# Two graph-attention layers: second block's adjacency in the setup, and a few steps of the layer change reordered

## The chip, the cores and the metric

The kernel runs on one core of a Trainium2 chip. The metric is the device time of one execution in microseconds, the median of several runs. TensorE (PE in the profile) multiplies matrices and transposes; VectorE (DVE), ScalarE (ACT) and GpSimd (POOL) work elementwise; SyncE (SP) only issues transfers and passes on waits. Each engine takes its own instructions in the order in which the program lists them, and semaphores make one engine wait for another. Matmuls write to PSUM banks, from which VectorE and ScalarE read.

## The reference, cut to what matters

Eight batches of 2048 nodes with 256 features pass through two layers; both use one adjacency matrix of 2048 x 2048. All arithmetic is float32.

```
# layer 0: attention in chunks, 4 heads of 64
h = relu(layernorm(x))
q, k, v = h Wq' + bq, h Wk' + bk, h Wv' + bv
for each of 8 chunks of 256 keys:                # softmax inside a chunk
    s = clip(q k' / 8, -10, 10);  s = -10 where adj == 0
    ctx += softmax(s) v
x = x + layernorm(ctx Wo' + bo + h) * gamma + beta
# layer 1: graph attention, one head
h = relu(layernorm(x)) W
e = leaky_relu(e_src[:, None] + e_dst[None, :], 0.01);  e = -1e9 where adj == 0
x = x + relu(softmax(e) h)
```

## The kernel before

**Blocks and steps.** The 2048 nodes of a batch are four blocks of 512 (`NNB`), each of four tiles of 128 (`TB`). Layer 0's attention walks 32 steps (`Attention.STEPS`), each one block of queries against one chunk of keys; every step is cut into two halves, `begin(f)` and `end(f)`, so that half steps are numbered 2f and 2f+1. Work that isn't attention is hung on half steps through the dictionary `todo`: a piece marked "first" runs at the head of its half step, one marked "pe" among TensorE's matmuls, the rest between the clips and the exponentials. The schedule is the order in the program; nothing reorders it.

**Adjacency.** A half row is 128 nodes x 1024 neighbours, 512 KB of int32. `load_rows` fetches it into one of four buffers; `missing_of` (L203, DVE) makes a mask of it; `turn_missing` (L211, PE, eight transposes into a bank of ps_t) turns it; `keep_bounds` (L215, ACT) writes it as int8 into `bounds[nb]`, the upper bound that `clip` (L440) uses for block nb. A block has eight half rows. Before, the setup treats block 0's half rows, two beside each projection block; `adjacency(nb)` spreads those of blocks 1, 2 and 3 over the half steps of batch 0's attention, block 1's from the first on. `store_bounds` saves the int8 blocks to DRAM for the later batches.

**Projections.** `Projection` computes q, k and v of a block: `load` brings x (two buffers), `stats`, `power` and `shift` give mean and scale (DVE, ACT, DVE), `norm(nb, t2)` normalizes half a block (L282, ACT), `turn` transposes it (L291, PE) and copies the two halves (L330 on DVE, L332 on ACT), `qk` multiplies (L344) and copies each product with its bias (L348, ACT); its `part` 0 is q, 1 is k. `values` is L358, with an addition on DVE (L363). With `ps_h` the products go to the large banks ps_s, otherwise by turns to ps_n and ps_t, two buffers of each.

**First attention step.** `Attention.early(0..2)` runs the first logits (L400), their clips (L440) and exponentials (L449) ahead of the step loop. In batch 0 all three stand behind the whole setup; in the others among the products of layer 1.

**The layer change.** When the attention of a batch ends, TensorE works through an order written by hand: for each of the four blocks (`zero`, `low`, `mid`, `last`) the output product (`output` L598, `take` L607), normalization, and then layer 1's transposes and copies (`ends(0)`: `turn1` L291, `keep1` L665 on ACT) and products with the weight W (`ends(1)`: `values` L672, `keep` L680 on ACT and L681 on DVE). Between them stand the next batch's projections (`ahead`). Then come the aggregation's inputs: `targets` (L764, L765), `sources` (L772 transposes, L776), `mean`, `weights` (L782 and L788 on DVE), and the aggregation itself (`products`, L805). The last batch has no `ahead`, and an order of its own. The sum over chunks is gathered by a transfer that adds (`gather`, L475), which the output products wait for.

**Fences.** Where two groups of matmuls write one bank, SyncE carries the wait (L372), in the same queue as its transfers.

Of the kernel before, what the change touches and what calls it, by code (L numbers as in the profile page):

```python
# [28 lines left out]
def gnn_two_layers(  # L29
# [26 lines left out]
    TB = NB // P  # L56
    NNB = N // NB
# [58 lines left out]
    bounds, bounds1 = {}, {}  # L116

    def bound_tile():
        return xpool.tile([P, NT, NB], I8, tag="bound", name="bound", bufs=2)
# [6 lines left out]
    def store_bounds(nb):  # L126
        nc.sync.dma_start(bound_d[nb], bounds[nb])
# [11 lines left out]
    def row_bcast(src, name):  # L139
        t = const.tile([P, F], F32, name=name)  # L140
        nc.sync.dma_start(t, row(src))
        return t
# [19 lines left out]
    def pe(piece):  # L162

        piece.kind = "pe"
        return piece
# [29 lines left out]
    def load_rows(t, half):  # L195
        rows = xpool.tile([P, HALF], I32, tag="x", name="rows", bufs=NNB)
        nc.sync.dma_start(rows, adj[t * P:(t + 1) * P, half * HALF:(half + 1) * HALF])
        return rows

    def missing_of(rows, t, half):  # L200

        z = work.tile([P, HALF], BF16, tag="hn", name="z", bufs=5)
        nc.vector.tensor_scalar(  # L203
            z, rows, 0.0, 0.0, op0=ALU.is_equal, op1=ALU.add, accum_out=missing[:, t, half:half + 1]
        )
        return z

    def turn_missing(z):
        pt = ps.tile([P, 8, P], BF16, tag="t", name="ps_z")
        for k in range(8):  # L210
            nc.tensor.transpose(pt[:, k, :], z[:, k * P:(k + 1) * P], ident_b)  # L211
        return pt

    def keep_bounds(pt, t, half):
        nc.scalar.activation(  # L215
            bounds[t // TB][:, half * 8:(half + 1) * 8, (t % TB) * P:(t % TB + 1) * P], pt, AF.Copy,
            scale=-2.0 * CLIP * SC, bias=CLIP * SC,
        )
# [622 lines left out]
    proj = Projection(0)  # L841
# [6 lines left out]
    bk_c = column(bk, "bk_c")  # L848
    bv_r = row_bcast(bv, "bv_r")
    proj.load(1)  # L850
    nearest = [(t, half) for t in range(TB) for half in range(2)]
    rows = {i: load_rows(*nearest[i]) for i in range(4)}
    proj.stats(0, range(TB))
    proj.power(0)
# [8 lines left out]
    bo_r = row_bcast(bo, "bo_r")  # L863
    gamma_r = row_bcast(gamma, "gamma_r")
    beta_r = row_bcast(beta, "beta_r")
    found = {i: missing_of(rows.pop(i), *nearest[i]) for i in range(2)}
    bounds[0] = bound_tile()
    proj.stats(1, range(TB))
    proj.power(1)
    proj.shift(1)  # L870
    for nb in range(NNB):
        for i in (2 * nb, 2 * nb + 1):
            keep_bounds(turn_missing(found.pop(i)), *nearest[i])
            if i + 4 < len(nearest):
                rows[i + 4] = load_rows(*nearest[i + 4])
        if nb + 1 < NNB:
            proj.norm(nb + 1, 0)
        proj.qk(nb, bank=ps_h)
        if nb + 1 < NNB:
            proj.norm(nb + 1, 1)  # L880
            for i in (2 * nb + 2, 2 * nb + 3):
                found[i] = missing_of(rows.pop(i), *nearest[i])
            if nb + 2 < NNB:
                proj.load(nb + 2)
            proj.turn(nb + 1, 0)
            proj.turn(nb + 1, 1)
            if nb + 2 < NNB:
                proj.stats(nb + 2, range(TB))
                proj.power(nb + 2)
                proj.shift(nb + 2)  # L890
        proj.values(nb)

    def layer1_weight():
        nc.sync.dma_start(w1s[:, :, 0:F], w1.rearrange("(c p) f -> p c f", p=P))

    def layer1_vector(i):
# [9 lines left out]

    once = {
        1: [lambda: raws.update(o=load_output_weight(wo)), layer1_weight],
        2: [lambda: store_bounds(0)],
        5: [pe(lambda: turn_weight(raws["o"], woT))],  # L910
        6: [lambda: layer1_vector(0)],
        7: [lambda: layer1_vector(1)],
        HALVES - PER: [find_lone],
    }
    for nb in range(1, NNB):
        for n, pieces in sorted(adjacency(nb).items()):
            once.setdefault(max((nb - 1) * PER + n, 0), []).extend(pieces)
    for piece in once.pop(0):
        piece()

    projs = {0: proj, 1: Projection(1)}
    projs[1].adder = nc.gpsimd
    att = Attention(proj)
    for part in range(3):
        att.early(part)
    unfinished = None
    for b in range(B):
        sd = small.tile([P, 2, NT], F32, tag="sd", name="sd", bufs=2)
# [2 lines left out]
        zero, low, mid, last = blocks  # L931
        ahead = projs.get(b + 1)
# [5 lines left out]
        def at(n, *pieces):  # L938
            todo.setdefault(n, []).extend(pieces)
# [7 lines left out]
        def fetch(of, nb):  # L947
            of[nb] = fetch_bounds(nb)
# [4 lines left out]
        if b == 0:  # L953
            for n, pieces in once.items():
                at(n, *pieces)

            for nb in range(NNB):
                n = 12 * nb + 5
                at(n - 2, lambda nb=nb: ahead.load(nb))
                for t in range(TB):  # L960
                    at(n + t, lambda nb=nb, t=t: ahead.stats(nb, [t]))
                at(n + 4, lambda nb=nb: ahead.power(nb))
                at(n + 5, lambda nb=nb: ahead.shift(nb))
        else:
            at(6, lambda: fetch(bounds, 1))
            at(PER + 4, lambda: fetch(bounds, 2))
            at(2 * PER + 4, lambda: fetch(bounds, 3))
# [39 lines left out]

        for block in blocks:
            block.adder = nc.vector
        for t in range(TB):  # L1010
            mid.stats1([t])
            low.values(t)
            low.keep(t)
        mid.power1()
        mid.shift1()
        if ahead:
            ahead.load(2)
            ahead.turn(1, 0)
            ahead.turn(1, 1)
            mid.norm1(0)  # L1020
            mid.norm1(1)
            ahead.norm(2, 0)
            ahead.values(0)
            last.output(0)
            last.output(1)
            last.take(0)
            last.take(1)
            ahead.norm(2, 1)
            ahead.load(3)
            mid.ends(0)  # L1030
            last.stats(range(TB))
            ahead.qk(1, 0)
            last.power()
            last.shift()
            last.scaled(range(TB))
            ahead.qk(1, 1)
            for t2 in range(2):
                last.gamma(t2)
                last.add(t2)
            for t in range(TB):  # L1040
                last.stats1([t])
                mid.values(t)
                mid.keep(t)
            last.power1()
            last.shift1()
            ahead.turn(2, 0)
            ahead.turn(2, 1)
            last.norm1(0)
            last.norm1(1)
            ahead.values(1)  # L1050
            zero.norm1(0)
            zero.norm1(1)
            ahead.norm(3, 0)
            ahead.qk(2, 0)
            zero.ends(0)
            zero.ends(1)
            ahead.norm(3, 1)
            ahead.qk(2, 1)
            ahead.turn(3, 0)
            ahead.turn(3, 1)  # L1060
            ahead.values(2)
            last.ends(0)
            last.ends(1)
            one.total()
            ahead.qk(3, 0)
            one.targets()
            one.sources(0)
            one.sources(1)
            ahead.qk(3, 1)
            weights(0)  # L1070
            one.mean()
            weights(1)
            ahead.values(3)
        else:
            mid.norm1(0)
            mid.norm1(1)
            one.targets(TB, 2 * TB)
            weights(0)
            mid.ends(0)
            last.output(0)  # L1080
            last.output(1)
            last.take(0)
            last.take(1)
            mid.ends(1)
            last.stats(range(TB))
            last.power()
            last.shift()
            weights(1)
            last.scaled(range(TB))
            one.targets(2 * TB, 3 * TB)  # L1090
            accs[0] = one.accumulators(0)
            early(0)
            for t2 in range(2):
                last.gamma(t2)
                last.add(t2)
            last.stats1(range(TB))
            last.power1()
            last.shift1()
            weights(2)
            last.norm1(0)  # L1100
            last.norm1(1)
            early(1)
            last.ends(0)
            last.ends(1)
            early(2)
            one.total()
            one.targets(3 * TB, NT)
            one.sources(1)
            weights(3)
            one.mean()  # L1110
            weights(4)

        far = projs[b + 2] = Projection(b + 2) if b + 2 < B else None
        for i, (nb, j4) in enumerate(pieces1):
# [19 lines left out]
            if far and i in (1, 3, 6, 9):  # L1134
                n = (1, 3, 6, 9).index(i)
# [3 lines left out]
            if ahead and i == len(pieces1) - 4:  # L1139
                att = Attention(ahead)  # L1140
# [36 lines left out]
```

## Time and profile before

| | us |
|---|---|
| median of 3 runs (lowest, highest) | 3664.26 (3662.63, 3664.51) |
| profiled span | 3661.2 |
| first attention matmul (L400) | 70.55 |
| first product of layer 1's aggregation (L805), batch 0 | 432.16 |
| the same, last batch | 3533.97 |

The page gives each engine's busy time with its share of the span. A timeline line gives the start in us, the length in us, the engine, the source line, the tiles written and read, how many instructions were merged, and in brackets how long the engine had stood idle and which engine and line released it. A line of the waits gives the total in us, how often, and the longest. TensorE's instructions overlap, so the spacing of two starts tells more than one instruction's length.

### The profile page before, as it was taken

What the parts mean: (1) busy time and instruction counts of PE and PEld (TensorE: products, weight loads), DVE (VectorE), ACT (ScalarE), POOL (GpSimd) and SP (SyncE); (2) the same over time, 40 slices, a digit from 0 to 9 for tenths busy, and PEclk for the clock granted to TensorE, in tenths of its full rate; (3) what the DMA queues carried; (4) which work ended last, traced back from release to release, by engine and by line L of the source; (5) the groups of instructions that cost most, each with busy time, mean ns of one, the idle gap of its engine ahead of it and who ended that gap; (6) DMA issues with size and microseconds to landing.
All of it is one profiled execution on the core that took longest, in us unless ns stands there. A gap on an engine that the chain in (4) does not pass through costs nothing.

```text
span 3661.2 us, 99422 instructions
## 1 busy us (share of the span) xinstructions
PE 3624.1 (99%) x43952; PEld 2209.7 (60%) x43952; DVE 2582.2 (71%) x3915; ACT 1959.1 (54%) x2975; POOL 1788.7 (49%) x1142
## 2 busy tenths in 40 slices
PE   8999999999999999999999999999999999999999
PEld 4444784547745577445775558645586555865468
DVE  4887577865778666776667856678576784767766
ACT  4777416773267732677236762367713766147650
POOL 0678016870178602786037850378404774048731
PEclk9999999999999999999999999999999999999999
DMA  4554113340134411343113431134312432124321
GB/s 141 137 129 111 41 52 83 83 109 26 67 80 89 94 42 52 83 100 82 47 47 83 100 76 46 59 77 95 75 52 59 88 88 59 47 53 89 71 59 35
DMA packets 116641, 274.83 MB, mean 75 GB/s; under 512 B 9968, under 2 KB 75248, under 8 KB 108016
## 3 DMA queue, kind: packets, MB, share of 16 engines
q0 software_dynamic: 32256, 117.45, 17.6%
q1 hardware_dynamic: 83952, 151.01, 12.1%
q8 instruction: 344, 5.64, 0.6%
q14 instruction: 89, 0.73, 0.1%
HBM read 130.03 MB, written 20.97 MB: 41 GB/s over the span
## 4 chain that ended last, share of the span: by engine, by line
PE 95%; DVE 2%; ACT 1%; DMA 1%; issue 0%; POOL 0%; POOLq 0%; SPq 0%; DVEq 0%; ACTq 0%
PE ps_s L400 24%; PE ps_n L416 23%; PE ps_s L805 12%; PE ps_t L428 6%; PE ps_n L805 6%; PE ps_t L805 6%; PE ps_t L598 3%; PE ps_s L344 2%; PE ps_n L344 2%; PE ps_t L344 2%; PE ps_t L672 2%; PE ps_t L358 1%; PE ps_n L672 1%; PE ps_n L358 1%; PE ps_t L291 1%; DMA ctxT<-prod 1%
## 5 line engine op out<-in xcount | busy, mean ns | idle before, releaser
L455 POOL TENSOR_TENSOR both<-e 128x1024 f32<-128x1024 f32 x512 | 1217.8, 2407 | 667.7 <-PE ps_s L400 269.9
L440 DVE SCALAR_TENSOR_TENSOR e<-ps_s,bound 128x1024 f32<-128x1024 f32 x1024 | 1219.4, 1220 | 384.8 <-PE ps_s L400 383.8
L400 PE MATMUL ps_s<-q,k 64*32 64x512 f32 x16384 | 1364.9, 590 | 2.8 <-DVE e L440 2.6
L449 ACT ACTIVATE e<-e 128x1024 f32<-128x1024 f32 x1024 | 1050.6, 1049 | 560.8 <-DVE e L440 540.5
L416 PE MATMUL ps_n<-e,v 64*32 64x512 f32 x16384 | 1164.0, 590 | 2.4 <-DVE prod L470 2.4
L416 PEld LDWEIGHTS ps_n<-e,v 64*32 64x32 f32 x16384 | 447.0, 107 | 501.7 <-issue 395.5
L400 PEld LDWEIGHTS ps_s<-q,k 64*32 64x32 f32 x16384 | 433.5, 106 | 460.3 <-issue 325.8
L822 POOL TENSOR_TENSOR x<-x,r 128x256 f32<-128x256 f32 x128 | 98.5, 769 | 1148.3 <-DVE rz L815 1017.4
L428 PE MATMUL ps_t<-both,ones 64*32 64x512 f32 x4096 | 537.5, 591 | 1.0 <-SPq L372 0.5
L805 PE MATMUL ps_s<-g,w 128*128 128x257 f32 x2048 | 448.6, 380 | 0.0
L470 DVE TENSOR_TENSOR prod<-ps_n,rz 128x512 f32<-128x512 f32 x448 | 288.7, 686 | 189.3 <-PE ps_n L416 85.1
L805 PEld LDWEIGHTS ps_s<-g,w 128*128 128x128 f32 x2048 | 387.8, 190 | 55.5
L788 DVE SCALAR_TENSOR_TENSOR w<-bound,w 128x1024 f32<-128x1024 int8 x256 | 313.7, 1225 | 8.7
L805 PE MATMUL ps_n<-g,w 128*128 128x257 f32 x1024 | 292.4, 382 | 0.0
L782 DVE TENSOR_SCALAR w<-src,cd 128x512 f32<-128x512 f32 x512 | 265.3, 561 | 36.2 <-ACT src L776 35.8
L805 PE MATMUL ps_t<-g,w 128*128 128x257 f32 x1024 | 289.8, 380 | 0.0
L460 ACT ACTIVATE rz<-ps_t 128x512 f32<-128x512 f32 x256 | 152.5, 596 | 172.3 <-PE ps_t L428 92.6
L475 POOL DMA_DIRECT2D ctxT<-prod x224 | 194.2, 867 | 52.5 <-DVE prod L470 49.0
L805 PEld LDWEIGHTS ps_n<-g,w 128*128 128x128 f32 x1024 | 192.2, 190 | 43.8 <-issue 17.6
L805 PEld LDWEIGHTS ps_t<-g,w 128*128 128x128 f32 x1024 | 193.9, 189 | 28.2
L428 PEld LDWEIGHTS ps_t<-both,ones 64*32 64x32 f32 x4096 | 121.1, 106 | 93.7 <-SPq L372 53.0
L461 ACT ACTIVATE rz<-rz 128x512 f32<-128x512 f32 x256 | 161.4, 631 | 8.1
(129 smaller groups left out, 2854.0 us busy)
## 6 DMA issues: line engine op xcount, KB each, us to landing
ctxT<-prod POOLq DMA_DIRECT2D x224, 512.0 KB, 4.9
bound<-bound_d SPq DMA_DIRECT2D x60, 1024.0 KB, 5.3
xp<-in_x_dram SPq DMA_DIRECT2D x60, 512.0 KB, 4.8
rows<-in_adj_dram SPq DMA_DIRECT2D x32, 512.0 KB, 5.3
x<-in_x_dram SPq DMA_DIRECT2D x32, 512.0 KB, 5.3
out_dram<-x SPq DMA_DIRECT2D x31, 512.0 KB, 2.9
bound_d<-bound SPq DMA_DIRECT2D x4, 1024.0 KB, 6.0
out_dram<-x SPq DMA_DIRECT2D x4, 128.0 KB, 1.7
```

The lines of the kernel that those rows point to most:

```text
L344: nc.tensor.matmul(pp, w[:, di, do * P:(do + 1) * P], self.hT[nb][:, di, :], start=di == 0, stop=di == FC - 1,)
L400: nc.tensor.matmul(self.s[n, o][c * Q:(c + 1) * Q, kt, :], self.k[p][rows, at:at + Q], self.q[p][rows, nb * NB:(nb + 1) * NB], start=True, ...
L416: made.append(nc.tensor.matmul(self.num[n, c][h * Q:(h + 1) * Q, :], self.v[rows, j * KT + kt, at:at + Q], self.e[n, p][rows, i * KT + kt, :],
L428: nc.tensor.matmul(self.total[n][h * Q:(h + 1) * Q, :], ones[rows, :], self.both[n, h // 2][rows, h % 2, :], start=half == 1, stop=half == 0,)
L440: nc.vector.scalar_tensor_tensor(self.e[n, p][:, i * KT:(i + 1) * KT, :], self.s.pop((n, o)), -CLIP * SC, bounds[nb][:, j * KT:(j + 1) * K ...
L449: nc.scalar.activation(e, e, AF.Exp, scale=1.0 / SC)
L455: nc.gpsimd.tensor_tensor(self.both[n, p], e[:, 0], e[:, 1], op=ALU.add)
L470: nc.vector.tensor_tensor(dst[:, c, :], self.num.pop((n, c)), self.rz[n], op=ALU.mult)
L475: nc.gpsimd.dma_start(self.ctxT[nb], self.prod.pop(n), accum_op=ALU.add)
L782: nc.vector.tensor_scalar(w[:, i, :], self.src[nb], self.cd[:, 0, j:j + 1], self.cd[:, 1, j:j + 1], op0=ALU.mult, op1=ALU.max,)
L788: nc.vector.scalar_tensor_tensor(two, bounds1[nb][:, j - 1:j + 1, :], 0.0, two, op0=ALU.is_gt, op1=ALU.mult)
L805: nc.tensor.matmul(accs[t][:, 0:F + 1], w[:, i, t * P:(t + 1) * P], g[:, j, :], start=j == 0, stop=j == NT - 1,)
```

## The change

It does four things. The setup treats the half rows of block 0 and of block 1, four beside each projection block instead of two, with q and k of a block parted (`find` makes masks and loads the row four places on, `bound` turns and keeps). The three early parts of batch 0's first attention step go among the projections of its last block. In the last batch, block `low`'s products run together before block `mid` is normalized, and block `last`'s output product goes ahead of `mid`'s transposes. In the layer change of the other seven batches two pieces of projection go between a block's transposes and its products. The statistics of batch 1, which are taken during batch 0, move from every twelfth half step to every fourth, into the room that block 1's half rows leave.

```diff
-    nearest = [(t, half) for t in range(TB) for half in range(2)]
+    nearest = [(t, half) for t in range(2 * TB) for half in range(2)]
...
+    find(0, 1)
+    for nb in range(2):
+        bounds[nb] = bound_tile()
     proj.stats(1, range(TB))
     proj.power(1)
     proj.shift(1)
-    for nb in range(NNB):
-        for i in (2 * nb, 2 * nb + 1):
-            keep_bounds(turn_missing(found.pop(i)), *nearest[i])
-            if i + 4 < len(nearest):
-                rows[i + 4] = load_rows(*nearest[i + 4])
-        if nb + 1 < NNB:
-            proj.norm(nb + 1, 0)
-        proj.qk(nb, bank=ps_h)
-        if nb + 1 < NNB:
-            proj.norm(nb + 1, 1)
-            for i in (2 * nb + 2, 2 * nb + 3):
-                found[i] = missing_of(rows.pop(i), *nearest[i])
-            if nb + 2 < NNB:
-                proj.load(nb + 2)
-            proj.turn(nb + 1, 0)
-            proj.turn(nb + 1, 1)
-            if nb + 2 < NNB:
-                proj.stats(nb + 2, range(TB))
-                proj.power(nb + 2)
-                proj.shift(nb + 2)
+    for nb in range(NNB - 1):
+        bound(4 * nb, 4 * nb + 1)
+        proj.norm(nb + 1, 0)
+        proj.qk(nb, 0, ps_h)
+        find(4 * nb + 2, 4 * nb + 3)
+        proj.norm(nb + 1, 1)
+        bound(4 * nb + 2, 4 * nb + 3)
+        proj.qk(nb, 1, ps_h)
+        find(4 * nb + 4, 4 * nb + 5)
+        if nb + 2 < NNB:
+            proj.load(nb + 2)
+        proj.turn(nb + 1, 0)
+        proj.turn(nb + 1, 1)
+        if nb + 2 < NNB:
+            proj.stats(nb + 2, range(TB))
+            proj.power(nb + 2)
+            proj.shift(nb + 2)
         proj.values(nb)
+    bound(12, 13)
+    proj.qk(NNB - 1, 0, ps_h)
+    att = Attention(proj)
+    att.early(0)
+    find(14, 15)
+    proj.qk(NNB - 1, 1)
+    att.early(1)
+    bound(14, 15)
+    proj.values(NNB - 1)
+    att.early(2)
...
-        2: [lambda: store_bounds(0)],
+        2: [lambda: store_bounds(0), lambda: store_bounds(1)],
...
-    for nb in range(1, NNB):
+    for nb in range(2, NNB):
         for n, pieces in sorted(adjacency(nb).items()):
...
-                n = 12 * nb + 5
-                at(n - 2, lambda nb=nb: ahead.load(nb))
+                n = 4 * nb + 4
+                at(n - 3, lambda nb=nb: ahead.load(nb))
...
             zero.ends(0)
-            zero.ends(1)
             ahead.norm(3, 1)
             ahead.qk(2, 1)
+            zero.ends(1)
             ahead.turn(3, 0)
             ahead.turn(3, 1)
             ahead.values(2)
             last.ends(0)
+            ahead.qk(3, 0)
             last.ends(1)
             one.total()
-            ahead.qk(3, 0)
             one.targets()
             one.sources(0)
...
         else:
+            mid.stats1(range(TB))
+            low.ends(1)
+            mid.power1()
+            mid.shift1()
             mid.norm1(0)
             mid.norm1(1)
             one.targets(TB, 2 * TB)
             weights(0)
-            mid.ends(0)
             last.output(0)
             last.output(1)
             last.take(0)
             last.take(1)
+            mid.ends(0)
             mid.ends(1)
```

More of the change, by code (lines that the diff above doesn't have):

```diff
@@ L865, in gnn_two_layers, with find, bound @@
     beta_r = row_bcast(beta, "beta_r")
-    found = {i: missing_of(rows.pop(i), *nearest[i]) for i in range(2)}
-    bounds[0] = bound_tile()
+    found = {}
+    def find(*parts):
+        for i in parts:
+            found[i] = missing_of(rows.pop(i), *nearest[i])
+            if i + 4 < len(nearest):
+                rows[i + 4] = load_rows(*nearest[i + 4])
+    def bound(*parts):
+        for i in parts:
+            keep_bounds(turn_missing(found.pop(i)), *nearest[i])
+    find(0, 1)
+    for nb in range(2):
+        bounds[nb] = bound_tile()
     proj.stats(1, range(TB))
@@ L914, in gnn_two_layers @@
     }
-    for nb in range(1, NNB):
+    for nb in range(2, NNB):
         for n, pieces in sorted(adjacency(nb).items()):
             once.setdefault(max((nb - 1) * PER + n, 0), []).extend(pieces)
-    for piece in once.pop(0):
-        piece()
     projs = {0: proj, 1: Projection(1)}
     projs[1].adder = nc.gpsimd
-    att = Attention(proj)
-    for part in range(3):
-        att.early(part)
     unfinished = None
@@ L1009, in gnn_two_layers @@
             block.adder = nc.vector
[L1010 to L1015, printed above, removed]
-        if ahead:
+        if ahead:
+            for t in range(TB):
+                mid.stats1([t])
+                low.values(t)
+                low.keep(t)
+            mid.power1()
+            mid.shift1()
             ahead.load(2)
@@ L1074, in gnn_two_layers @@
         else:
+            mid.stats1(range(TB))
+            low.ends(1)
+            mid.power1()
+            mid.shift1()
             mid.norm1(0)
```

## The prediction

> **What bounds the kernel now.** I read the page first, then the list of waits, then the timeline at the three places that the change touches.
>
> ```profile
> PE 3624.1 (99%) x43952; PEld 2209.7 (60%) x43952; DVE 2582.2 (71%) x3915; ACT 1959.1 (54%) x2975; POOL 1788.7 (49%) x1142
> ...
> PE 95%; DVE 2%; ACT 1%; DMA 1%; issue 0%; POOL 0%; POOLq 0%; SPq 0%; DVEq 0%; ACTq 0%
> ```
> TensorE is busy for 99% of the span and is 95% of the chain that ended last. So an edit pays only where TensorE stands still, or where a matmul waits in a way that stretches a group. The change removes no matmul. It can win only holes in TensorE's row.
>
> ```profile
> PE ps_t L291 <- ACT hn L282: 9.5, 12, 3.2
> PE ps_t L672 <- ACT hT L665: 6.1, 15, 0.5
> ```
> These lines of TensorE's waits (total, times, longest) name two holes: layer 1's products (L672) wait for the copy of their transposed input (15 times, which is 7 layer changes x 2 and one more), and transposes (L291) wait for the normalization. Here is one layer change, TensorE alone:
>
> ```profile
> 402.42 0.60 PE L291 MATMUL ps_n<-ident,hn 128*128 128x128 f32 x4
> 403.50 1.28 PE L672 MATMUL ps_t<-w1s,hT 128*128 128x258 f32 x4 [0.48 <-ACT hT L665]
> ...
> 407.23 1.88 PE L344 MATMUL ps_t<-hT,wkT 128*128 128x512 f32 x4
> ...
> 415.43 0.60 PE L291 MATMUL ps_n<-ident,hn 128*128 128x128 f32 x4
> 416.37 1.28 PE L672 MATMUL ps_t<-w1s,hT 128*128 128x258 f32 x4 [0.34 <-ACT hT L665]
> ...
> 420.10 1.88 PE L344 MATMUL ps_t<-hT,wqT 128*128 128x512 f32 x4
> ```
> The setup, where each block's transposes wait for ScalarE:
>
> ```profile
> 24.94 0.38 PE L291 MATMUL ps_t<-ident,hn 128*128 128x128 f32 x2
> 26.37 0.33 PE L291 MATMUL ps_t<-ident,hn 128*128 128x128 f32 x1 [1.05 <-ACT hn L282]
> ...
> 27.46 1.89 PE L358 MATMUL ps_t<-wvT,hT 128*128 128x256 f32 x8
> ```
> And the end of the last batch:
>
> ```profile
> 3518.15 1.03 PE L672 MATMUL ps_n<-w1s,hT 128*128 128x258 f32 x4
> 3522.33 1.95 PE L291 MATMUL ps_t<-ident,hn 128*128 128x128 f32 x4 [3.15 <-ACT hn L282]
> ...
> 3524.93 3.62 PE L598 MATMUL ps_t<-woT,ctxT 128*128 128x256 f32 x8
> 3528.34 2.29 PE L598 MATMUL ps_n<-woT,ctxT 128*128 128x256 f32 x8
> ...
> 3533.97 14.04 PE L805 MATMUL ps_s<-g,w 128*128 128x257 f32 x64
> ```
> The reader is to see, beside the hole of 3.15 us, that the first eight output products (L598) take 3.41 us to the next group, where eight of the same shape take 1.73 us at an ordinary layer change. TensorE is slow just after the hole.
>
> [...] 3.41 against 1.73 us is a factor of two, after 3.15 us of idleness and then sparse transposes; the 1.05 us holes of the setup are followed by nothing slow. [...] so a copy queued behind a waiting instruction waits too, which is how I place every wait below.
>
> **Part 1: the layer change (seven times).** The products of block 0 go behind the second half of block 2's projections (k), and those of block 3 behind the first half of block 3's (q). Nothing is added. First hole: the transposes' last group starts at 402.42 and needs 0.44 us (the group before it began at 401.98), so TensorE could go on at 402.86; L672 starts at 403.50, 0.64 us later, and its 16 matmuls take 3.73 us (403.50 to 407.23), where four such groups without a wait take 3.49 us (390.73 to 394.22 in the same view): 0.24 more. Second hole: 415.87 to 416.37 is 0.50, and again 3.73 instead of 3.49. Sum 0.64 + 0.24 + 0.50 + 0.24 = 1.62 us. In the new order a projection half (2 x 1.72 us) stands between transposes and products; the two copies need 2 x 0.8 us on ScalarE, so they are hidden. Does the projection find its banks? It takes the banks of the projection half before the transposes, whose copies end at 402.13 and 402.87, against a need at 402.86 and 404.6. On ScalarE the normalization (1.08 us) now stands ahead of the k copies; they end near 405.7 and 407.2, and the products need those banks at 408 and 408.9. After block 3's products the transposes of the sources follow at once and read only other blocks' columns; the targets on ScalarE wait 0.8 us for the last column, and behind them stand the source exponentials. The weights then start about 2.1 us after the sources' transposes, 1.8 before, and are needed 8.6 us after them: hidden. So 7 x 1.62 = **11.3 us gained**. Bounds: 8 (if half of the 0.24s and a little more stay) to 12.
>
> **Part 2: the setup.** Removed: the transposes of a block take 24.94 to 27.46 = 2.52 us instead of 0.88, since ScalarE normalizes after four copies; now the second normalization stands between the q and k halves. 1.64 x 3 = 4.9 us gone. Moved in: block 1's eight half rows. Each costs DVE 1.21 us (L203), TensorE 0.5 (16 transposes in 1.0), ScalarE 1.01 (L215). TensorE's work only moves: 4 us more in the setup, 4 us less later. Per block ScalarE has about 10 us, DVE 10, TensorE 13.5 (7.0 projections, 3.5 values, 0.9 transposes, 2.0 masks): TensorE stays the fullest, so what matters is order.
>
> The added wait: SyncE's queue. In the new order two row loads stand before each load of x, and each must wait until the mask of the row four places before has freed its buffer. I walk the queues: DVE makes masks 2 and 3 from 18.0 to 20.3 as before, then masks 4 and 5 to 22.7; the load of x for block 2 goes out at 23 instead of 15.33 and lands at 28.7 (4.8 us from the page's DMA part, and 0.9 for the row loads ahead of it, each 1.45 us as 512 KB at the 361 GB/s of the stretch 10 to 20). Statistics take 2.35 us (27.83 to 30.05), the scale factors on ScalarE and the shift 1.1, the value addition behind them on DVE 0.69: 32.9. That addition frees the bank of the next block's second mask. TensorE: q to 21.5, masks 22.5, k 26.0, transposes 26.9, values 30.35, first mask 30.8: a stall of 2.1 us, where before it was 0.35. For block 3 the same walk gives x out at 38.9, landed at 43.9, the addition at 47.9, TensorE there at 46.2: 1.75. So of 4.9 us some 3.2 come back.
>
> The early attention: its first 32 matmuls now lie between q and k, which hides their clips; before, 1.40 and 0.56 us were lost there, and 0.66 and 0.36 on the masks. But the third part still waits for clip (0,2), which stands on DVE behind the last value addition: 2.1 us; the values wait for a mask copy that stands on ScalarE behind two exponentials, 1.2 us; the first logits wait 0.5 us for a q copy and the second step's 1.2 us for a clip. That is 5 us, hardly less than before. In times: q of block 3 from 61.9 (60.08 before) to 65.3, first logits to 67.7, k to 71.2, second logits 72.9, masks 73.9, values from 75.1 to 78.65, its addition 79.5, clip (0,2) 80.8, the second step's first logits 81.6, its last from 83.2 to 84.6; before they ended at 84.34. By then eight more half rows are done instead of four (the others came at 108.59 and 117.56): 2.2 us gained.
>
> Later in batch 0 the statistics of batch 1 move from every twelfth to every fourth half step. Before, their last two blocks fell together with block 3's masks, with single holes: 0.56 us at 201.07, 0.48 at 251.07, and near 265. They now fall where block 1's masks were: 1.8 us gained. Part 2 together: **4 us gained**. Best case 9 (x arrives in time), worst a loss of 5 (each load of x 3 us later still, and the tail's waits doubled).
>
> **Part 3: the last batch's end.** The output products go ahead of block 2's transposes. They need the last accumulating transfer into ctxT: issued at 3517.14, 4.8 us to land as the one before (3510.61), so 3522.0; the hole is 3519.0 to 3522.0, hardly shorter. But dense products follow it at once instead of transposes that come one by one. If the clock stays up: 16 products 3.46 to 3525.4; transposes 0.88 to 3526.3; a wait of 0.6 for the copy (and for the takes on DVE, which come after the weights at 3526.0 and end at 3527.4); products 3.7, to 3530.6, instead of 3533.97. **3.4 us gained**; what follows hangs on these products through DVE's chain and moves with them. If the clock falls: 1 us.
>
> **The rivals.** (a) Main line: 3664.3 - 11.3 - 4 - 3.4 = 3645.6. (b) The same with the clock falling at the end: 3648; [...] against it, the 2.4 us of sparse work near 3549 slowed nothing. (c) Setup takes back what it wins, the x loads late: +9 against the main line, 3654.6; for it, DMA engines are full from 10 to 20 us. (d) Setup without new stalls: 3640.6; for it, TensorE is the fullest engine there. (e) The other side: the reordered projections wait for their banks and the hole of 0.9 us only moves, once in each change (7 x 0.9 = 6 more, none gained), the setup loses 5, the end gains nothing: 3664 + 6 + 5 = 3675; against it stand the copies' times of part 1.
>
> **How the numbers follow.** Chances: (a) 0.46, (b) 0.2, (c) 0.15, (d) 0.15, (e) 0.04. The likeliest is (a): 3645.6 us. The range must hold (a), (b), and most of (c) and (d): 3639 to 3655. Within 0.2% means above 3657: the upper part of (c) and some of (e), 0.06; slower 0.04; faster 0.9.
>
> **What would show it.** Right: no L672 behind L665 at the layer changes, spans between changes shorter by 1.6 us; in the setup, TensorE waiting for DVE's L363 instead of ACT's L282, second step's logits ending near 84 us; L598 ahead of L291 at the end, with 1.73 us for eight. Wrong: new waits of L344 at the changes, first attention later than 90 us, or L598 still at 3.4 us.

## The result and the profile after

| | before | after |
|---|---|---|
| median of 6 runs each, us (lowest, highest) | 3663.19 (3660.94, 3664.51) | 3653.97 (3649.28, 3656.7) |
| ratio, 95% interval | | 0.9973 [0.996, 0.9986] |
| profiled span, us | 3661.2 | 3650.6 |

The change makes the kernel faster, by 9.2 us where 18.7 were forecast. The time lies at the upper end of the range, beside rival (c), 3654.6: the setup takes back what it wins because the loads of x come late. TensorE's share of the span and of the chain that ended last is what it was (first two lines of the page on engines and of its chain):

```profile
PE 3613.9 (99%) x43952; PEld 2203.8 (60%) x43952; DVE 2581.0 (71%) x3915; ACT 1958.1 (54%) x2975; POOL 1788.5 (49%) x1142
...
PE 95%; DMA 2%; DVE 2%; ACT 1%; POOL 0%; issue 0%; SPq 0%; POOLq 0%; DVEq 0%; ACTq 0%
```

TensorE's waits (engine, tile and line, releaser: total us, times, longest) show what went and what came. The 15 waits of L672 are two, and the 9.5 us of L291 are 2.7. At the head stands one that was 0.4 us before, also in two waits: the transposes of masks wait for the value addition, 8.4 us now.

```profile
PE ps_z L211 <- DVE v L363: 8.4, 2, 5.9
...
PE ps_t L291 <- ACT hn L282: 2.7, 5, 1.5
PE ps_t L598 <- DMA ctxT<-prod: 2.6, 1, 2.6
...
PE ps_t L672 <- ACT hT L665: 0.7, 2, 0.3
```

Where the difference of the two spans arose, by the times at which some matmuls start:

| stretch | before, us | after, us | difference | forecast |
|---|---|---|---|---|
| start to the first L416 (context of the first step) | 84.34 | 92.81 | +8.47 | +0.3 |
| from there to batch 0's first L805 | 347.82 | 341.75 | -6.07 | -5.6 |
| from there to the last batch's first L805 | 3101.81 | 3087.51 | -14.30 | -13.1 |
| from there to the end | 127.23 | 128.52 | +1.29 | 0 |

The forecasts are those of the prediction: 84.6 instead of 84.34; 2.2 + 1.8 and one layer change of 1.62; six layer changes and 3.4 for the last batch's end. The second and third rows came about as forecast. The first did not. Here is the setup after, TensorE alone:

```profile
30.66 0.61 PE L211 MATMUL ps_z<-ident_b,z 128*128 128x128 bf16 x8
37.19 1.01 PE L211 MATMUL ps_z<-ident_b,z 128*128 128x128 bf16 x8 [5.91 <-DVE v L363]
37.99 4.83 PE L344 MATMUL ps_s<-hT,wqT 128*128 128x512 f32 x8
...
54.46 1.01 PE L211 MATMUL ps_z<-ident_b,z 128*128 128x128 bf16 x8 [2.48 <-DVE v L363]
55.27 4.72 PE L344 MATMUL ps_s<-hT,wqT 128*128 128x512 f32 x8
...
82.99 1.99 PE L358 MATMUL ps_t<-wvT,hT 128*128 128x256 f32 x8 [0.70 <-ACT bound L215]
...
88.63 2.19 PE L400 MATMUL ps_s<-q,k 64*32 64x512 f32 x24 [1.91 <-DVE e L440]
91.89 1.49 PE L400 MATMUL ps_s<-q,k 64*32 64x512 f32 x20 [1.07 <-DVE e L440]
```

Two holes stand in the places that were forecast, but of 5.91 and 2.48 us instead of 2.1 and 1.75, and the q projection after each takes 4.83 and 4.72 us, where the one without a hole takes 3.65. The granted clock is why: it stood at 0.50 from 33.52 to 40.35 and from 54.01 to 57.42, and at 1.00 between and behind. In this line (stretch, length, busy us of PE, PEld, DVE, ACT and POOL with their counts, granted clock, DMA share, GB/s) it is the third number from the end:

```profile
36.94:40.34 3.40, 3.15 (x11) 1.92 (x11) 3.40 (x7) 2.30 (x4) 0.00 (x0) 0.50 0.12 13
```

Follow the first hole back. VectorE:

```profile
33.30 0.43 DVE L259 BATCH_NORM_STATS2 stats<-xp 128x6 f32<-128x256 f32 x1 [5.63 <-DMA xp<-in_x_dram]
...
36.36 0.16 DVE L270 TENSOR_TENSOR krn<-krn,mv 128x4 f32<-128x4 f32 x1 [0.84 <-ACT krn L266]
36.44 0.69 DVE L363 TENSOR_TENSOR v<-ps_t,bv_r 128x512 f32<-128x512 f32 x1
```

VectorE stood idle for 5.63 us until block 2's x was there. The value addition, whose products were done at 29.10 and 30.83, stands behind the statistics in its order and starts at 36.44; when its first half ends, the bank is free and the mask's transposes start, at 37.19. SyncE's own queue says when that x was asked for:

```profile
14.93 9.33 SPq L197 DMA_DIRECT2D rows<-in_adj_dram  x6
24.35 0.39 SPq L151 DMA_DIRECT2D xp<-in_x_dram  x1
```

It went out at 24.35 and landed at 33.27. Ahead of it three row loads were still under way; by the trace they landed at 27.02, 29.06 and 30.33, in the order of their issue. In the trace the landing of each of these loads is reported in sixteen parts: fifteen parts of x were in by 31.71, and the last, 1.56 us later, is what VectorE waited for. Why it came so late no run here shows. The table by stretches gives the rate meanwhile (the second stretch runs on past the landing):

```profile
24.00:28.00 4.00, 4.00 (x18) 2.49 (x17) 0.69 (x1) 3.74 (x6) 0.00 (x0) 1.00 0.82 233
28.00:34.00 6.00, 3.27 (x22) 2.73 (x21) 0.67 (x3) 0.01 (x1) 0.00 (x0) 0.96 0.51 182
```

At the layer change and at the last batch's end the new order works as intended. A layer change (batch 0's), with no wait at all in TensorE's row:

```profile
406.45 0.60 PE L291 MATMUL ps_n<-ident,hn 128*128 128x128 f32 x4
406.88 1.88 PE L344 MATMUL ps_t<-hT,wkT 128*128 128x512 f32 x4
408.60 1.88 PE L344 MATMUL ps_n<-hT,wkT 128*128 128x512 f32 x4
410.32 1.03 PE L672 MATMUL ps_t<-w1s,hT 128*128 128x258 f32 x4
```

And the end of the last batch, where the output products follow the hole at full speed (1.80 us from one eight to the next, 3.41 before):

```profile
3509.82 1.03 PE L672 MATMUL ps_n<-w1s,hT 128*128 128x258 f32 x4
3513.43 1.97 PE L598 MATMUL ps_t<-woT,ctxT 128*128 128x256 f32 x8 [2.58 <-DMA ctxT<-prod]
3515.23 1.89 PE L598 MATMUL ps_n<-woT,ctxT 128*128 128x256 f32 x8
...
3522.07 14.04 PE L805 MATMUL ps_s<-g,w 128*128 128x257 f32 x64
3539.46 2.09 PE L672 MATMUL ps_t<-w1s,hT 128*128 128x258 f32 x4 [0.34 <-ACT hT L665]
```

The last line is the +1.29 of the table's last row: there the granted clock stood at 0.50 from 3539.01 to 3542.43, behind sparse transposes, and four products took 2.09 us instead of 1.03 or 1.28.

### The profile page after: what moved, and what is told of

Same layout as the page of the kernel before. It is cut to its first block, busy times and chain, and to the rows that moved or that the text cites. A ratio compares the mean times of both kernels' runs of the same rounds, so it can differ in the third digit from the quotient of the medians.

```text
span 3650.6 us, 99411 instructions
## 1 busy us (share of the span) xinstructions
PE 3613.9 (99%) x43952; PEld 2203.8 (60%) x43952; DVE 2581.0 (71%) x3915; ACT 1958.1 (54%) x2975; POOL 1788.5 (49%) x1142
## 4 chain that ended last, share of the span: by engine, by line
PE 95%; DMA 2%; DVE 2%; ACT 1%; POOL 0%; issue 0%; SPq 0%; POOLq 0%; DVEq 0%; ACTq 0%
PE ps_s L400 24%; PE ps_n L416 24%; PE ps_s L805 12%; PE ps_t L428 6%; PE ps_n L805 6%; PE ps_t L805 6%; PE ps_t L598 3%; PE ps_t L344 2%; PE ps_n L344 2%; PE ps_s L344 2%; PE ps_t L672 2%; PE ps_t L358 1%; PE ps_n L672 1%; PE ps_n L358 1%; DMA ctxT<-prod 1%; PE ps_t L291 1%
## 5 line engine op out<-in xcount | busy, mean ns | idle before, releaser
L416 PE MATMUL ps_n<-e,v 64*32 64x512 f32 x16384 | 1165.9, 590 | 1.6 <-DVE prod L470 1.3
L416 PEld LDWEIGHTS ps_n<-e,v 64*32 64x32 f32 x16384 | 443.1, 107 | 504.7 <-issue 400.7
L805 PE MATMUL ps_s<-g,w 128*128 128x257 f32 x2048 | 448.7, 380 | 0.0
L470 DVE TENSOR_TENSOR prod<-ps_n,rz 128x512 f32<-128x512 f32 x448 | 288.4, 685 | 188.5 <-PE ps_n L416 86.5
L805 PEld LDWEIGHTS ps_s<-g,w 128*128 128x128 f32 x2048 | 388.5, 190 | 54.9
L805 PE MATMUL ps_n<-g,w 128*128 128x257 f32 x1024 | 292.5, 382 | 0.0
L805 PE MATMUL ps_t<-g,w 128*128 128x257 f32 x1024 | 290.0, 380 | 0.0
L805 PEld LDWEIGHTS ps_n<-g,w 128*128 128x128 f32 x1024 | 192.6, 190 | 43.5 <-issue 17.6
L805 PEld LDWEIGHTS ps_t<-g,w 128*128 128x128 f32 x1024 | 194.1, 190 | 27.9
```

The source lines that it names most:

```text
L416: made.append(nc.tensor.matmul(self.num[n, c][h * Q:(h + 1) * Q, :], self.v[rows, j * KT + kt, at:at + Q], self.e[n, p][rows, i * KT + kt, :],
L470: nc.vector.tensor_tensor(dst[:, c, :], self.num.pop((n, c)), self.rz[n], op=ALU.mult)
L805: nc.tensor.matmul(accs[t][:, 0:F + 1], w[:, i, t * P:(t + 1) * P], g[:, j, :], start=j == 0, stop=j == NT - 1,)
```

## The experiments

My theory after the result: the layer change brings nearly all of the gain; the setup loses in its holes what its better order wins, and the holes come from the place of x's load in SyncE's queue. The rival: the setup loses by something else, the masks moved in or the early attention, and an earlier x changes nothing. Ratios are against the kernel before, timed on the same chip, with 95% intervals; "the first L416" is the end of the setup, 84.34 before and 92.81 after.

**x asked for first.** Edit, against after:

```diff
     for nb in range(NNB - 1):
+        if nb + 2 < NNB:
+            proj.load(nb + 2)
         bound(4 * nb, 4 * nb + 1)
...
         find(4 * nb + 4, 4 * nb + 5)
-        if nb + 2 < NNB:
-            proj.load(nb + 2)
```

> The changed kernel with one edit: in the setup the load of x for block nb+2 is issued at the head of a block's turn, ahead of that block's row loads. Theory (the x load waits in SyncE's queue behind row loads that wait for masks, and its late statistics hold the value additions and so the bank of the next mask): the holes of 5.91 and 2.48 us before the second mask of blocks 1 and 2 shrink to under 1 us each, the half-speed q projections after them (4.83 and 4.72 us) return to 3.65, the first L416 starts near 83 us instead of 92.81, and the time falls by 8 to 10 us against the changed kernel, to about 0.9948 of before. Rival (the masks themselves overfill VectorE, and the additions come late whatever x does): the holes keep 2 us or more each, the first L416 stays after 88 us, and the time falls by 4 us or less.

Measured: 3644.75 us, ratio 0.9954 [0.9942, 0.9967]. The load went out at 15.39 and landed at 22.17. Both holes are 0.18 us, and q is at full speed after each. The timeline of TensorE at the place of the first hole:

```profile
29.69 0.61 PE L211 MATMUL ps_z<-ident_b,z 128*128 128x128 bf16 x8
30.48 0.61 PE L211 MATMUL ps_z<-ident_b,z 128*128 128x128 bf16 x8 [0.18 <-DVE v L363]
30.93 3.65 PE L344 MATMUL ps_s<-hT,wqT 128*128 128x512 f32 x8
```

The first L416 starts at 82.93. The masks and the early attention are as in after, so the rival falls. Of the 9.9 us, 1.0 lies ahead of the first hole (29.69 against 30.66) and has nothing to do with it: the late x cost some 9 us of the setup. In the tail the clock fell in this profile (granted clock 0.5 from 77.15 to 83.97), so that the last logits took longer (24 of them 3.21 us and 20 of them 2.79, in after 2.19 and 1.49): at their start, 76.66 instead of 88.63, the lead had been 12.0 us. By the timings x first is worth some 7 us (0.9954 against 0.9973), and these two intervals just overlap. The time is also within 1 us of the 3645.6 which the prediction gave for the change itself; that is in part chance, since this kernel lacks holes that the prediction had allowed for (2.1 and 1.75 us) and lost about 2 us to the clock in its tail.

**x behind the first two row loads.** A middle dose: against after, the load goes ahead of `find(4 * nb + 4, 4 * nb + 5)`.

```diff
         proj.qk(nb, 1, ps_h)
-        find(4 * nb + 4, 4 * nb + 5)
         if nb + 2 < NNB:
             proj.load(nb + 2)
+        find(4 * nb + 4, 4 * nb + 5)
```

> The changed kernel with the load of x one place earlier: ahead of the second pair of masks and row loads of a block, behind the first pair. Theory (the late landing is made of the row loads ahead of it: some 1.2 us each for the mask that must free the buffer, and about 2 us each of the transfer engines' time, since they moved 182 to 233 GB/s there and not 361): x for block 2 issues near 22 us and lands near 28 to 29 instead of 33.27, the hole of 5.91 us shrinks to 1 to 2, that of 2.48 to under 1, and the time lies between the changed kernel and a1_x_first, nearer to the latter, ratio 0.9955 to 0.9962. Rival (the engines are full of earlier row loads whatever stands ahead in the queue): x lands after 31 us and the hole keeps 4 us or more.

Measured: 3651.03 us, ratio 0.9967 [0.9953, 0.9981]; x out at 20.75, landed at 29.16.

```profile
33.07 1.01 PE L211 MATMUL ps_z<-ident_b,z 128*128 128x128 bf16 x8 [3.12 <-DVE v L363]
33.88 6.20 PE L344 MATMUL ps_s<-hT,wqT 128*128 128x512 f32 x8
```

The landing was as expected, the hole longer (3.12 us against 1 to 2) and the ratio above the 0.9955 to 0.9962 that were expected. The q projection behind it took 6.20 us, 2.55 more than at full speed: nearly as much again as the hole. With the other two kernels it makes a row of three doses: x lands at 33.27, 29.16, 22.17; the first hole is 5.91, 3.12, 0.18; the first L416 starts at 92.81, 87.71, 82.93. The first of them began its masks some 1 us later than the other two. The setup alone (below) didn't, and fits the row: 31.34, 5.45 and 90.58. The ratios follow in order (0.9973, 0.9967, 0.9954), though the intervals of the first two overlap widely.

**The layer change alone.** Against before:

```diff
             zero.ends(0)
-            zero.ends(1)
             ahead.norm(3, 1)
             ahead.qk(2, 1)
+            zero.ends(1)
...
             last.ends(0)
+            ahead.qk(3, 0)
             last.ends(1)
             one.total()
-            ahead.qk(3, 0)
```

> The kernel before with the layer change's reordering alone. Theory (1.62 us of TensorE's wait hidden in each of seven changes, and nothing in return): 11 us faster than before, ratio 0.9970, no L672 behind L665 at those changes. Rival (part of it comes back as waits elsewhere in the batch): 4 to 7 us, ratio 0.998 to 0.999.

Measured: 3649.83 us, ratio 0.9973 [0.9962, 0.9984], 10.5 us against the 3660.32 of before on the same chip. In TensorE's waits the 15 of L672 have become one of 0.3 us. These two moved lines are worth about what the whole change is worth.

**The setup alone.** After, with the layer change and the last batch's end as before:

```diff
             zero.ends(0)
+            zero.ends(1)
             ahead.norm(3, 1)
             ahead.qk(2, 1)
-            zero.ends(1)
...
-            mid.stats1(range(TB))
-            low.ends(1)
-            mid.power1()
-            mid.shift1()
```

> The kernel before with the setup's part alone (second block's masks, early attention parts, and the moved statistics of batch 1). Theory (the setup loses 8.5 us up to the first L416 and batch 0 wins about 4.4 back): 2 to 6 us slower than before, ratio 1.0005 to 1.0016. Rival (the setup is neutral, and the difference between forecast and result lies in the layer change): within 1.5 us of before.

Measured: 3660.39 us, ratio 1.0001 [0.9993, 1.001]. The first L416 starts at 90.58, 6.2 later than before; from the last turn of the output weight (L190, soon after) to the first L805, batch 0 takes 338.56 us instead of 343.31, 4.75 won back. A loss was expected and none can be timed: the interval runs from a gain of 2.6 us to a loss of 3.7, and the profile has the first L805 of batch 0 1.7 us late. So the setup is worth nothing that shows. The holes were 5.45 and 3.72:

```profile
53.66 0.61 PE L211 MATMUL ps_z<-ident_b,z 128*128 128x128 bf16 x8 [3.72 <-DVE v L363]
54.10 3.65 PE L344 MATMUL ps_s<-hT,wqT 128*128 128x512 f32 x8
```

Here q kept full speed after a hole of 3.72 us; after the hole of 2.48 us in the change itself it didn't.

**The last batch's end alone.** Against before, only the last branch:

```diff
         else:
+            mid.stats1(range(TB))
+            low.ends(1)
...
             weights(0)
-            mid.ends(0)
             last.output(0)
...
+            mid.ends(0)
             mid.ends(1)
```

> The kernel before with the last batch's end alone. Theory (the clock stays up behind a hole of under 3 us): 3.4 us faster, ratio 0.9991, L598's first eight at 1.7 to 2.0 us. Rival (the clock falls there, or another half-speed stretch comes later in the same stage): 1 us faster at most.

Measured: 3659.08 us, ratio 0.9999 [0.9991, 1.0008]: too little to time. By the profile, this time the clock fell in the output products, behind a hole of 2.61 us (3.17 us for the second eight of them; in after, behind a hole of 2.58, the two eights took 1.97 and 1.89):

```profile
3519.12 2.41 PE L598 MATMUL ps_t<-woT,ctxT 128*128 128x256 f32 x8 [2.61 <-DMA ctxT<-prod]
3521.32 3.17 PE L598 MATMUL ps_n<-woT,ctxT 128*128 128x256 f32 x8
```

From the last products ahead of the hole to the first L805 it took 13.97 us (3515.48 to 3529.45); before it was 15.82 (3518.15 to 3533.97), in after 12.25 (3509.82 to 3522.07). So the order is worth 1.9 us where the clock falls and 3.6 where it stays. It fell behind this hole in this profile and in those of x asked for first, of the reordered tail and of the old statistics below (13.96, 13.96 and 13.79 us; their first eight output products took 3.65, 3.12 and 3.48 us behind holes of 2.60), and stayed up in after's. With x behind two row loads it fell earlier, behind a hole of 1.63 us.

**The early attention alone.** Before, with the three early parts among the last block's projections and nothing else:

```diff
-        proj.qk(nb, bank=ps_h)
+        if nb + 1 < NNB:
+            proj.qk(nb, bank=ps_h)
+        else:
+            proj.qk(nb, 0, ps_h)
+            att = Attention(proj)
+            att.early(0)
+            proj.qk(nb, 1)
+            att.early(1)
...
+    att.early(2)
```

> The kernel before with the early attention parts among the last block's projections alone; block 1's masks stay in the attention. Theory (the third part's clips still stand behind the value additions, so the waits only change their place): the first L416 within 1.5 us of 84.3, ratio 0.9996 to 1.0004. Rival (hiding the first clips behind k is worth the 3 us of holes that were seen there): the first L416 near 81, ratio 0.9992.

Measured: 3663.77 us, ratio 1.0007 [0.9999, 1.0016]; the first L416 at 85.25 instead of 84.34. The clips' waits only change place:

```profile
77.36 1.92 PE L400 MATMUL ps_s<-q,k 64*32 64x512 f32 x16 [2.01 <-DVE e L440]
```

**The tail in another order.** If the third part waits because its clip stands behind the value addition, and the values wait for a mask's copy, then the third part should go ahead of the values and the values among the first half steps. Edit, against x asked for first:

```diff
     att.early(1)
     bound(14, 15)
-    proj.values(NNB - 1)
     att.early(2)
...
+            at(4, pe(lambda: projs[0].values(NNB - 1)))
```

> The run with x first (a1_x_first) with one more edit: the third early part goes ahead of the last block's values, and those values become a piece of the first half step of the loop. Theory (the holes of 0.70, 1.92 and 1.33 us at the end of the setup are the values waiting for a mask copy and the logits waiting for clips that stand behind the value additions on VectorE): all three fall under 0.8 us, the first L416 comes within 1 us of the place where its work then stands, and the time falls by 3 to 5 us against a1_x_first, ratio to before 0.9942 to 0.9946. Rival (the clips are too slow for TensorE there whatever stands ahead of them): the holes stay, ratio 0.995 or more.

Measured: 3639.25 us (3637.95 to 3639.8), ratio 0.9941 [0.9929, 0.9954]. The first L416 starts at 77.35, 5.6 earlier than in the kernel it builds on, of which about 2 us are the clock that fell in that kernel's tail and stayed up here (32 logits in 1.95 us). One short wait is left:

```profile
68.72 1.07 PE L211 MATMUL ps_z<-ident_b,z 128*128 128x128 bf16 x16
70.10 1.92 PE L400 MATMUL ps_s<-q,k 64*32 64x512 f32 x16 [0.32 <-DVE e L440]
71.95 3.72 PE L358 MATMUL ps_t<-wvT,hT 128*128 128x256 f32 x16
75.61 1.95 PE L400 MATMUL ps_s<-q,k 64*32 64x512 f32 x32
77.35 1.92 PE L416 MATMUL ps_n<-e,v 64*32 64x512 f32 x32
```

It has the lowest median of the study, 21 us below before. Against x asked for first (0.9954) the intervals overlap; the waits that are gone are the surer sign.

**The statistics of batch 1 back in their old place.** Against x asked for first:

```diff
-                n = 4 * nb + 4
-                at(n - 3, lambda nb=nb: ahead.load(nb))
+                n = 12 * nb + 5
+                at(n - 2, lambda nb=nb: ahead.load(nb))
```

> The run with x first with the statistics of batch 1 back on every twelfth half step. Theory (they then fall together with the masks of blocks 2 and 3, and cost the 1.8 us named in the forecast): 1 to 2.5 us slower than a1_x_first, ratio to before 0.9958 to 0.9961, and from the transposes of the output weight (L190) to the first L805 338.5 to 340 us instead of 337.7. Rival (the place of the statistics makes no difference, and what batch 0 wins comes from the masks alone): within 0.5 us.

Measured: 3644.3 us, ratio 0.9961 [0.9948, 0.9973], beside 0.9954 for the kernel that it undoes: not told apart. By the profile, the last turn of the output weight to the first L805 takes 338.17 us against 337.66: 0.5 us, and not the 1.8 of the forecast.

**The last batch's hole filled.** Against the reordered tail, work that waits for nothing is put ahead of the output products:

```diff
+            at(STEPS2 + 3, lambda: weights(0))
...
-            weights(0)
+            accs[0] = one.accumulators(0)
+            early(0)
+            weights(1)
             last.output(0)
             last.output(1)
...
+            early(1)
+            weights(2)
```

> b1_tail with another order at the last batch's end: the first weights are made two half steps earlier, while VectorE waits for the accumulating transfer, and their products go into the hole ahead of the output product; the later weights and block last's statistics move forward with them. Theory (the hole before L598 is the landing of the last accumulating transfer, so only work that doesn't need it can fill it): no wait of L598 for the transfer, 3 to 6 us faster than b1_tail, ratio to before 0.993. Rival (the hole only moves behind the products, to block last's transposes, since VectorE's chain sets that time): within 1 us of b1_tail.

Measured: 3642.52 us, ratio 0.9953 [0.9941, 0.9966], 3.3 us slower than the kernel it builds on. The wait of L598 is gone, and two others have come:

```profile
3495.78 2.09 PE L672 MATMUL ps_n<-w1s,hT 128*128 128x258 f32 x4 [4.39 <-DVE prod L470]
...
3540.00 1.14 PE L805 MATMUL ps_s<-g,w 128*128 128x257 f32 x4 [1.46 <-DVE w L788]
```

The weights, made earlier, now stand ahead of the last step's scaling (L470) in VectorE's order, and TensorE waits for that scaling. The hole moved and grew; what looked like free work took the place of work that the end hangs on.

## Why the prediction was right and where it was wrong

**Part 1, the layer change: right.** 11.3 us were forecast. Done alone it brought 10.5, interval 5.9 to 13.9 (0.0016 and 0.0038 of 3660.32). The waits named are gone and no wait of L344 has come at the layer changes, so rival (e) falls.

**Part 2, the setup: the mechanism right, one term mis-sized, one missing.** The failed step is "lands at 28.7". It took 0.9 us for what stood ahead of the load and the median 4.8 for the load itself, 5.7 together; it took 8.9 (24.35 to 33.27). The landings came in the order of issue, 27.02, 29.06, 30.33 and 33.27. Three row loads and x, 2.1 MB, had to come through, where I had two row loads at the 361 GB/s of an earlier stretch; and the last sixteenth came 1.56 us behind the rest. The median was the wrong price, and the trace of before could have said so: there the same load took 6.9 us, issued at 15.33 and landed at 22.22, the longest of the setup. The other part of "lands at 28.7", "goes out at 23", was right for the order: with the setup alone x went out at 23.12 and landed at 31.34, 2.6 late. In the profile of the change the first masks started 1.1 us later (14.96 against 13.84 before and 13.87 with the setup alone, so it is no part of the change), and x went out at 24.35.

The whole was 4.6 us late, of which 3.8 show in the first hole (5.91 against 2.1) and 0.7 in the second. The missing term is the clock, granted at 0.50 there: behind the two holes the q projections took 1.18 and 1.07 us more than without, and the mask's transposes ahead of them 0.36 more each (1.01 instead of 0.61 us long, 0.80 instead of 0.44 to the next start). The late start of the masks had shrunk to 0.4 when the first q ended (21.95 against 21.5). That is 3.8 + 0.7 + 2.3 + 0.7 + 0.4 = 7.9 us; up to block 3's q the forecast was off by 7.5 (69.43 against 61.9), and by 8.2 at the first L416. The experiment with x first shows the same from the other side: no hole, no slow q, some 9 us back.

The rest of Part 2 held. The waits of the tail were put at 0.5, 1.2, 2.1 and 1.2 us, 5.0 together; they were 0.8 (2.77 us instead of 1.95 in the first logits), 0.70, 1.91 and 1.07, 4.5 together. That the early parts among the projections save nothing by themselves was right too. What batch 0 wins back was put at 2.2 + 1.8 = 4.0 and measured as 4.75 in the setup alone, but the split was wrong by the profile: about 0.5 for the moved statistics, the rest for the half rows. No timed difference confirms the 0.5, so that split stays open.

**Part 3, the last batch's end: both cases seen.** With the clock up 3.4 us were forecast and 3.6 measured, with the clock down 1 and 1.9. The chance was too high: I took the first for likelier, which was an estimate (before shows one hole of about that length in the last batch, 3.15 us, with the clock at 0.50 behind it, from 3522.33 to 3529.15), and in the six profiles described here with the new end and no filling it came once; in four the clock fell behind this hole, in one ahead of it. What I had set against a falling clock, that the sparse work near 3549 slowed nothing, held in before but not in after: behind the same work, at 3539.46, four products ran at half speed there (2.09 us, 1.28 in before), which is the +1.29. The timed experiment can't resolve either, so the mean worth of this part stays open.

**The sum.** 10 (Part 1), about nothing instead of 4 (Part 2), and 1.9 to 3.6 (Part 3) would give about 12 to 14 where 9.2 were timed; parts timed alone have intervals of several us, so the parts and the whole agree no better than that. The measured 3653.97 is inside the range because the range was drawn to hold most of rival (c), and (c), late loads of x, is what came, though it had been given 0.15. The likeliest time, 3645.6, was 8 us too low.

## What to carry to other kernels

SyncE's queue issued in the order of the program: x, which waited for nothing, went out at 24.35 behind row loads that wait for a buffer, and at 15.39 ahead of them. Such a load belongs ahead of loads that wait for a buffer to come free; price it by the bytes still ahead of it in its queue (behind three row loads it took 8.9 us), and by how long it took in the same stage before (6.9 us), not by its median (4.8). Follow a late load through every engine's order to the buffer it holds back: here 5.63 us without x on VectorE reached TensorE as a hole of 5.91 us, through a value addition queued behind statistics. Before filling a hole with ready work, see what that work stands ahead of on its own engine: with the hole of 2.60 us filled, one of 4.39 came ahead of it.

## What the runs showed of the hardware that was not expected

The length of a hole didn't decide whether the clock fell after it. Matmuls behind holes of 2.48 (after), 2.60 and 2.61 us (x first, end alone) ran at half speed at least in part (q in 4.72 us, eight output products in 3.65 and 3.17); behind 2.58 (after) and 3.72 us (setup alone) they did not (1.97 for eight output products, 3.65 for q). The shortest was 1.63 us, in the last batch with x behind two row loads: TensorE's timeline there shows both slow groups.

```profile
3506.63 1.83 PE L672 MATMUL ps_n<-w1s,hT 128*128 128x258 f32 x4 [1.63 <-DVE prod L470]
3508.26 1.93 PE L672 MATMUL ps_t<-w1s,hT 128*128 128x258 f32 x4
3509.98 1.22 PE L672 MATMUL ps_n<-w1s,hT 128*128 128x258 f32 x4
```

Four such products take 1.03 to 1.14 us at full speed, behind a hole of 1.23 us in after too. What went with the fall more closely is where the hole lay. In the traces of before and after the granted clock changes only at moments that are whole multiples of 3.41 us apart. In after, whose record of it begins at 19.87, it falls to 0.50 at 33.52, rises at 40.35, falls at 54.01, rises at 57.42, falls at 3539.01, rises at 3542.43 and falls at 3648.24: between these lie 6.83, 13.65, 3.41, 3481.60 (1020 times 3.4133), 3.41 and 105.81 us (31 times). In before it falls at 3522.33, rises at 3529.15 and falls at 3658.86: 6.83 and 129.71 us (2 and 38 times). Cut the run at these moments, and the two cases part (columns as above; the first view is from after, the second from the setup alone):

```profile
50.59:54.00 3.41, 1.39 (x13) 1.07 (x12) 2.44 (x10) 1.10 (x4) 0.00 (x0) 1.00 0.00 0
54.01:57.42 3.41, 2.96 (x11) 1.93 (x11) 3.41 (x7) 2.42 (x4) 0.00 (x0) 0.50 0.13 14
```

```profile
48.45:51.86 3.41, 1.49 (x13) 1.16 (x12) 1.95 (x8) 0.00 (x0) 0.00 (x0) 1.00 0.04 15
51.86:55.27 3.41, 1.61 (x11) 1.07 (x11) 2.57 (x7) 2.59 (x6) 0.00 (x0) 1.00 0.00 0
55.28:58.68 3.40, 3.40 (x23) 1.95 (x22) 2.78 (x7) 2.48 (x6) 0.00 (x0) 1.00 0.54 169
```

The hole of 2.48 us left TensorE 1.39 us of work in one such stretch, and the next ran at 0.50. The hole of 3.72 us was divided over two, 1.49 and 1.61 us of work were left, and the clock stayed. Other such stretches at full clock, by the time without a matmul: it fell after 3.14 (before, 3518.91 to 3522.32), 2.24 (after, 30.11 to 33.52), 1.91 and 1.27 (x first, in its tail and in the last batch), 1.63 (x behind two row loads) and 1.25 us (after, 3535.60 to 3539.01), and not after 1.72 (after, 3511.71 to 3515.12) or 1.40 (before, 71.45 to 74.86), nor after the 1.92 and 1.80 of the setup alone. So the idle time of a stretch didn't decide alone either, and the rest stays open.

In after, the hole of 2.48 us cost about half its length again: 1.07 us more in the q projection behind it.

Timings of one kernel spread by more than the differences between some of these versions: after's six runs lie from 3649.28 to 3656.7 us, the three lowest with a mean granted clock of 0.998 and the three highest with 0.996 to 0.997. The size fits: a mean clock lower by 0.001 to 0.002 is worth, by my estimate, 4 to 7 us of 3650. Which places of the program it fell in, no run here shows.
